# A graph network of four layers: the next entry's neighbour sums moved behind this entry's z sums, z, y and output kept in one tile, the second layer's bias folded into constants

## The chip, the cores and the metric

The kernel runs on one core of a Trainium2 chip. The metric is the device time of one execution in microseconds (us); the profile is one further execution, recorded by the hardware profiler. Engines are named as in the profile: PE is the matrix engine and PEld its weight loads, DVE the vector engine, ACT the scalar engine, POOL GpSimd, SP the sync engine, which here only issues transfers.

## The reference

The input x has 32 entries of 512 nodes by 256 features (float32). adj is one sparse 512 by 512 matrix that all entries share. Four layers follow one another; the first and the last have the same form with weights of their own:

```python
def L0(h):                      # and L3
    pre_u, pre_v = h @ W1[:d], h @ W1[d:]
    S = sigmoid(relu(pre_u[:, u] + pre_v[:, v] + b1) @ W2 + b2)    # one number for each pair u, v
    a_t = einsum('buv,bud->bvd', S * adj, h)
    m_t = einsum('uv,bud->bvd', adj, h) * h
    return beta1 * h + beta2 * (a_t @ Wa + ba) + beta3 * (m_t @ Wm + bm)
def L1(z):
    return z + relu((adj @ z) @ W.T + b)                           # y
def L2(y):
    feats = y @ W1.T
    f1 = feats @ W2 + b2
    coefs = softmax(leaky_relu(f1[:, :, None] + f1[:, None, :]) + adj)
    return coefs @ feats + bias2 + y
```

S is needed only where adj is not zero, so the kernel makes it for the edges alone.

## The kernel before

Entries are worked in eight groups of four (`NB`). Every group passes through five streams of small pieces:

- `first`: turns the four inputs round on PE, writes them to DRAM as `xT`, and writes `pre_u` and `pre_v` of all nodes to a DRAM table (`pre`).
- `edges` of layer 0: 36 items. An item fetches table rows by an indirect transfer (POOL, L612), adds the other node's rows (DVE, L691), applies relu and W2 (DVE L707, or DVE L699 with ACT L677), the sigmoid, and puts the values into a DRAM array `cells` by an indirect transfer (POOL, L606).
- `middle`: the rest of layer 0, layers 1 and 2, and `pre` of layer 3, one entry after the other (`middle_one`).
- `edges` of layer 3, then `last`: the rest of layer 3 and the output.

All streams are woven into one order by `weave`: each piece has a due time on a scale in which a group takes 1.0, and pieces are written out in order of due time. The due times of the middle's pieces are spread by `middle_shares`, a hand-written list of weights; those of the edges by `edge_times`. Pieces of `first` and `last` are "fill": they wait in a list and are written out behind those pieces of the middle that yield True. The framework then arranges the instructions of each engine, mostly in this order; an instruction can be taken ahead of others where its inputs and its buffer are ready by the framework's reckoning. Each engine, and each queue of transfers, then works strictly in its own order.

An entry of `middle_one` consists of these steps, by the lines of the kernel before:

1. `mhT`: 16 PE rows adj x h (L45; a float32 matmul of the code is two rows in the trace) and two DVE products with hT (L755). These are the neighbour sums of the layer.
2. The sums for z: 16 PE rows hWa x `flat` (L845) and 8 rows with mhT (L852); ACT scales hT in place (L850), DVE adds the sums (L853, two instructions). z lies in the tile of hT.
3. zW: 16 PE rows with z as the stationary side (L866), copied by ACT (L870).
4. adj x zW (16 rows, L45), relu with bias by ACT (L876) into `yT`, plus z by DVE (L877).
5. feats (L888, copied by ACT L896 into a tile that shares the tag `mhT0`), a softmax of four chunks (ACT L912 and L916, DVE L913 to L918), four turns (L957), of which two have the next entry's hWa (L744) in front of them in the text, and coefs x feats (16 rows), with the sum x2 by DVE (L935).
6. x2 goes to DRAM (SP, L937). `flat` of the next entry is copied by ACT (L814, four copies) out of `SA`, the four tiles of layer 0's S * adj, into the tile that coefs had. Then `pre` for layer 3 (16 PE rows; DVE L579, ACT L580, DVE L582 and L583 for each of four chunks), and x2 is turned (L946).

`flat` and coefs share one buffer (tag `eT`). h (`h1`), hT (`hT1`), `hWa0` and `mhT0` have one buffer each. At a group's start the text loads SA (POOL, L732), h and hT (SP, L821 and L825), and makes hWa of the first entry. Group 0 is a special case ("given"): its hWa and mhT are made in `middle_before`. PSUM has seven banks for all products (`ps`) and one for f1.

Of the kernel before, what the change touches and what calls it, by code (L numbers as in the profile page):

```python
# [47 lines left out]
class Model:  # L48
# [90 lines left out]
    def others_loads(self, raw):  # L139
        nc, a, const = self.nc, self.a, self.const  # L140
        self.b_1 = self.column("L1_gnn_b")
        self.w2 = self.column("L2_gnn_W2")
        self.b2 = self.bcast("L2_gnn_b2", 1)
        self.bias2 = self.column("L2_gnn_bias2")
        self.W1_1, self.W1_2 = raw([P, DC, D]), raw([P, DC, D])
        nc.scalar.dma_start(self.W1_1, a["L1_gnn_W"].rearrange("(c p) d -> p c d", p=P))
        nc.scalar.dma_start(self.W1_2, a["L2_gnn_W1"].rearrange("(c p) i -> p c i", p=P))
        self.twob2 = const.tile([P, 1], F32, name="twob2")
        self.WT_1 = const.tile([P, DC, D], F32, name="WT_1")
        self.WT_2 = const.tile([P, DC, D + 1], F32, name="WT_2")  # L150

    def others(self, psum):
# [9 lines left out]
        for c in range(DC):  # L162
            pq = psum()[:, 0:1]
            mm(nc, pq, [(self.W1_2[:, r, c * P : (c + 1) * P], self.w2[:, r, :]) for r in range(DC)])
            nc.vector.tensor_copy(self.WT_2[:, c, D : D + 1], pq)
        yield

# [52 lines left out]
class Edges:  # L220
# [28 lines left out]
    def build(self, counts, adjT, lists, psum, big, tmp):  # L249
# [66 lines left out]
        for c in (0, 2, 1, 3):  # L316
            if c == 1:
# [21 lines left out]
                for k in range(2 * PANELS):  # L339
                    if k < 2:  # L340
                        gots.append(two[:, k, :])
                    else:
                        gots.append(tmp.tile([P, 2 * N], F32, name=f"got{k}", tag=("h1", "hT1")[k - 2]))
                    index = bass.IndirectOffsetOnAxis(ap=inode[:, k : k + 1], axis=0)
# [74 lines left out]
class Sparse:  # L419
# [3 lines left out]
    def __init__(self, ctx, m, counts, xr, outr, B):  # L423
# [18 lines left out]
        self.ps_f1 = pool("ps_f1", 1, space=PSUM)  # L442
        self.later, self.bigs, self.given, self.marks = None, 0, None, {}

# [120 lines left out]
    def pre(self, g, b, hT):  # L565
# [3 lines left out]
        for c in range(NC):  # L569
# [10 lines left out]
            nc.scalar.copy(puv[:, 1, :], pp[:, D:])  # L580
            both = self.small.tile([P, D], F32, name="both", bufs=1)
            nc.vector.tensor_tensor(both, pp[:, D:], puv[:, 0, :], ALU.add)  # L582
            nc.vector.scalar_tensor_tensor(  # L583
# [31 lines left out]

    def edges(self, g, spare=()):

# [28 lines left out]
        def fetch(n):  # L646
# [11 lines left out]
            if tag := tags[n % len(tags)]:  # L658
                rows = self.act.tile([P, GROUP], F32, name="rows_more", tag=tag)
            else:  # L660
# [61 lines left out]
        while ready:  # L722
            put()
        yield

# [52 lines left out]
    def middle_before(self, g0, i):  # L778

        self.given = []  # L780
        for b in range(NB):
            h, hT = self.fresh(i + b)
            hT = hT()
            both = self.big(F32, 2048, 3).rearrange("p (k n) -> p k n", k=2)
# [7 lines left out]

    def middle(self, g0, g3, i):


        SA = self.load(g0, 0)
        given, self.given = self.given, None
        h, hT = self.fresh(i, given)
        hT = hT()
        hWa = None  # L800
        if not given:
            for hWa in self.hWa(g0, hT, 0):
                yield
        flat = self.flat(SA, 0)
        for b in range(NB):
            keep = [h, hT, hWa, flat]
            yield from self.middle_one(g0, g3, b, i + b, SA, keep, given)
            h, hT, hWa, flat = keep
        self.settle()
# [6 lines left out]

    def fresh(self, i, given=None):
        h = None
        if not given:
            h = self.act.tile([P, NC, D], F32, name="h1")  # L820
            self.nc.sync.dma_start(h, self.xr[i])  # L821

        def turned():
            hT = self.act.tile([P, DC, N], F32, name="hT1")
            self.nc.sync.dma_start(hT, self.xT[i])  # L825
            return hT

        return h, turned

    def middle_one(self, g0, g3, b, i, SA, keep, given):  # L830
        nc, m, w = self.nc, self.m, g0.w
        act, small, psum = self.act, self.small, self.psum
        h, hT, hWa, flat = keep
        if given:
            hWa, mhT = given[b]
        else:
            for mhT in self.mhT(h, hT, 0):
                yield
        zT = hT
# [8 lines left out]
        for c, pz in enumerate(sums):  # L848
# [5 lines left out]
            yield c == DC - 1  # L854
        more = b < NB - 1
        if more:
            keep[0], turned = self.fresh(i + 1, given)

        zW = act.tile([P, NC, D], F32, name="zW", tag="hWa0")
        halves = [(0, psum()), (2, psum())]  # L860
        for d in range(DC):
# [9 lines left out]
            yield d == DC - 1  # L871
        yT = act.tile([P, DC, N], F32, name="yT")
        for c in range(DC):
            py = psum()
            mm(nc, py, [(zW[:, r, c * P : (c + 1) * P], self.adjT[:, r, :]) for r in range(NC)])
            nc.scalar.activation(yT[:, c, :], py, AF.Relu, bias=m.b_1[:, c, :])  # L876
            nc.vector.tensor_tensor(yT[:, c, :], yT[:, c, :], zT[:, c, :], ALU.add)  # L877
            yield c == DC - 1

        feats = act.tile([P, NC, D + 1], F32, name="feats", tag="mhT0")  # L880
        eT = act.tile([P, NC, N], F32, name="eT")
        if more:
            keep[1] = turned()
            ahead = None if given else self.hWa(g0, keep[1], 0)
        pns = [psum() for _ in range(NC)]
# [14 lines left out]
        fcol = small.tile([P, NC, 1], F32, name="fcol", bufs=1)  # L900
        nc.vector.tensor_scalar(fcol, feats[:, :, D : D + 1], m.twob2, None, ALU.add)
        f1 = self.ps_f1.tile([P, N], F32, name="f1")
# [21 lines left out]
        for ic in (NC - 2, NC - 1):  # L924
            if more and ahead:
                keep[2] = next(ahead)
                yield
            self.put_back(eT, ic, exs[ic])
            yield True
        xT = yT  # L930
        for c in range(DC):
            cs = slice(c * P, (c + 1) * P)
            pv = psum()
            mm(nc, pv, [(feats[:, jc, cs], eT[:, jc, :]) for jc in range(NC)])
            nc.vector.scalar_tensor_tensor(xT[:, c, :], pv, m.bias2[:, c, :], yT[:, c, :], ALU.add, ALU.add)  # L935
            yield c == DC - 1
        nc.sync.dma_start(self.x2T[i], xT)  # L937
        if more:
            keep[3] = self.flat(SA, b + 1)
        yield from self.pre(g3, b, xT)  # L940
# [126 lines left out]

def middle_shares(given):


    hWa = [] if given else [1.7, 1.7]
    shares = list(hWa)
    for b in range(NB):
        more = hWa if b < NB - 1 else []
        shares += [] if given else [2.8, 2.8]
        shares += [3.4, 3.4, 1.0, 2.7]
        shares += [1.7, 3.4, 2.8, 4.5] + [0.9] * NC
        shares += [0.4, 0.4, 0.4, 1.0, 0.4, 1.0] + more + [1.5, 1.5]
        shares += [2.8, 4.5] + [0.4] * NC + [0.5, 0.5]
    return shares + [0.1]  # L1080
# [3 lines left out]
def sparse_path(ctx, m, counts, xr, outr, B):  # L1084
# [10 lines left out]
    for t in range(last + 1):  # L1095
# [17 lines left out]
        if t == last:  # L1113
# [4 lines left out]
            (sp.first(g0, t * NB), first, "fill"),  # L1118
            (sp.edges(g0, ("yT", "mhT0", "hWa0") if t == 0 else ()), edges0, ""),
            (sp.middle(g0, g3, t * NB), spread(middle_shares(t == 0), start, end), "main"),  # L1120
            (sp.edges(g3, ("yT", "h1", "hT1") if t == last else ()), edges3, "free"),
        ]
# [245 lines left out]
```

## Time and profile before

| | |
|---|---|
| three runs | 3113.56, 3114.72, 3128.83 us; median 3114.72 us |
| span of the profiled execution | 3112.8 us (its own execution time is not listed apart from the runs above) |
| busy, share of the span | PE 87%, DVE 74%, POOL 49%, ACT 43%, PE weight loads 53% |
| mean granted PE clock | 0.942 of full speed |
| one group in the steady part | about 358 us; the middle's first sums for z start at 239.8 us, the last entry's coefs x feats ends at 2881.9 us |

A row of the waits names who waited for whom: microseconds in total, times, longest. A row of the groups of instructions gives busy time and the mean of one in ns, then the engine's idle time before it and what ended most of it. In a timeline a bracket at a row's end is the engine's idle time just before it.

### The profile page before, as it was taken

How to read it: one execution, taken by the hardware profiler on the slowest of the kernel's cores; microseconds unless marked ns; L12 is line 12 of the kernel's file. 1: busy time of each engine (PE TensorE's matmuls, PEld its weight loads, DVE VectorE, ACT ScalarE, POOL GpSimd, SP SyncE). 2: the span in 40 equal slices, each digit the busy share in tenths (PEclk: the TensorE clock that was granted, in tenths of full speed). 3: DMA queues.
4: the chain of work that ended last, by engine and by line, in shares of the span. 5: the costliest groups of instructions: out<-in, count | busy, mean ns of one | idle time of the engine just before them, and what ended most of it. 6: DMA issues, size and time to landing. Idle time of an engine off the chain costs nothing. (4 is left out here: it accounts for less than half of the span.)

```text
span 3112.8 us, 32475 instructions
## 1 busy us (share of the span) xinstructions
PE 2713.5 (87%) x8645; PEld 1639.7 (53%) x8646; DVE 2302.9 (74%) x6027; ACT 1337.7 (43%) x4101; POOL 1531.2 (49%) x1328
## 2 busy tenths in 40 slices
PE   6367878889998899989998899989998899879957
PEld 3133444446654566446654565545654466546636
DVE  6964877888689776988489785888679795772761
ACT  3553454444344433444354442544345343443440
POOL 2561553656345552656346562555436563450461
PEclk9688889999999999999999999999999999999979
DMA  8774657776778757776678766787578766551753
GB/s 278 267 238 151 210 164 242 248 261 214 225 214 293 220 189 227 245 263 216 210 212 258 236 196 211 243 266 234 177 225 273 247 220 200 182 183 49 231 196 115
DMA packets 302719, 679.40 MB, mean 218 GB/s; under 512 B 52672, under 2 KB 170944, under 8 KB 294336
## 3 DMA queue, kind: packets, MB, share of 16 engines
q0 software_dynamic: 122688, 414.40, 42.6%
q1 hardware_dynamic: 160880, 225.62, 22.0%
q10 hardware_dynamic: 18960, 37.24, 3.2%
q8 instruction: 70, 1.15, 0.1%
q14 instruction: 121, 0.99, 0.1%
HBM read 531.12 MB, written 146.01 MB: 218 GB/s over the span
## 5 line engine op out<-in xcount | busy, mean ns | idle before, releaser
L606 POOL DMA_INDIRECT cells<-s,cell x576 | 686.4, 1192 | 747.0 <-DMA cells<-s,cell 388.5
L612 POOL DMA_INDIRECT rows<-table,iv x552 | 667.6, 1209 | 619.9 <-DMA table<-puv 150.5
L691 DVE TENSOR_TENSOR rows<-rows,mine 128x1024 f32<-128x1024 f32 x552 | 667.4, 1217 | 191.7 <-DMA rows<-table,iv 173.3
L677 ACT ACTIVATE rows<-rows 128x256 f32<-128x256 f32 x1088 | 439.8, 407 | 506.6 <-DVE rows L699 477.3
L45 PE MATMUL pst<-adj,h 128*128 128x512 f32 x1024 | 452.6, 594 | 0.3 <-PE pst L946 0.3
L707 DVE SCALAR_TENSOR_TENSOR rows<-rows,L_gnn_W2bc 128x256 f32<-128x256 f32 x1120 | 415.0, 417 | 1.8
L45 PE MATMUL pst<-L_gnn_Wa,hT 128*128 128x256 f32 x1024 | 261.3, 406 | 104.8 <-DMA hT<-xT 56.2
L699 DVE SCALAR_TENSOR_TENSOR rows<-rows,L_gnn_W2bc 128x1024 f32<-128x1024 f32 x272 | 329.7, 1214 | 0.3
L45 PEld LDWEIGHTS pst<-adj,h 128*128 128x128 f32 x1024 | 193.4, 191 | 223.3 <-issue 219.4
L45 PEld LDWEIGHTS pst<-L_gnn_Wa,hT 128*128 128x128 f32 x1024 | 204.8, 205 | 151.8 <-issue 85.1
L45 PE MATMUL pst<-eT,feats 128*128 128x512 f32 x512 | 230.9, 604 | 13.0 <-ACT eT L958 13.0
L866 PE MATMUL pst<-WT,hT 128*128 128x256 f32 x512 | 155.1, 470 | 96.0 <-DVE hT L853 96.0
L45 PE MATMUL pst<-adjT,zW 128*128 128x512 f32 x512 | 227.7, 597 | 3.8 <-ACT zW L870 3.8
L1006 PEld LDWEIGHTS pst<-hWa,SA 128*128 128x128 f32 x896 | 213.8, 328 | 7.7 <-issue 4.1
L1006 PE MATMUL pst<-hWa,SA 128*128 128x256 f32 x896 | 216.8, 398 | 0.0
L814 ACT COPY flat<-SA 128x512 f32<-128x512 f32 x128 | 137.7, 1127 | 165.9 <-PE pst L45 83.7
L677 ACT ACTIVATION_READ_ACCUMULATOR rows<-rows 128x1 f32 x1088 | 205.4, 189 | 0.0
L845 PE MATMUL pst<-flat,hWa 128*128 128x512 f32 x448 | 196.8, 592 | 0.0
L866 PEld LDWEIGHTS pst<-WT,hT 128*128 128x128 f32 x512 | 121.4, 242 | 136.6 <-DVE hT L853 107.1
L579 DVE TENSOR_TENSOR puv<-pst,bc_L_gnn_b 128x256 f32<-128x256 f32 x256 | 104.4, 414 | 95.8 <-DMA table<-puv 58.6
L580 ACT COPY puv<-pst 128x256 f32<-128x256 f32 x256 | 93.5, 370 | 180.6 <-DVE puv L579 162.7
L45 PEld LDWEIGHTS pst<-eT,feats 128*128 128x128 f32 x512 | 97.2, 193 | 127.5 <-issue 109.4
(172 smaller groups left out, 3984.4 us busy)
## 6 DMA issues: line engine op xcount, KB each, us to landing
table<-puv SPq DMA_DIRECT2D x256, 256.0 KB, 5.7
SA<-cells POOLq DMA_DIRECT2D x64, 1024.0 KB, 7.2
h<-in_x_dram SPq DMA_DIRECT2D x64, 512.0 KB, 6.5
mine<-table SPq DMA_DIRECT2D x64, 512.0 KB, 5.5
hT<-xT SPq DMA_DIRECT2D x36, 512.0 KB, 5.0
h<-x2s SPq DMA_DIRECT2D x36, 512.0 KB, 4.4
xT<-hT ACTq DMA_DIRECT2D x32, 512.0 KB, 6.1
x2T<-yT SPq DMA_DIRECT2D x32, 512.0 KB, 5.5
```

What stands on the lines that cost most here:

```text
L45: nc.tensor.matmul(out, lhsT, rhs, start=(n == 0), stop=(n == len(pairs) - 1))
L579: nc.vector.tensor_tensor(puv[:, 0, :], pp[:, 0:D], w["b1bc"], ALU.add)
L606: self.nc.gpsimd.indirect_dma_start(out=g.cells[half], out_offset=bass.IndirectOffsetOnAxis(ap=at, axis=0), in_=s, in_offset=None)
L612: self.nc.gpsimd.indirect_dma_start(out=rows, out_offset=None, in_=g.table, in_offset=bass.IndirectOffsetOnAxis(ap=at, axis=0))
L677: self.behind(nc.scalar.activation(part, part, AF.Identity, accum_out=g.s[:, k, b : b + 1]))
L691: self.behind(nc.vector.tensor_tensor(rows, rows, other, ALU.add))
L699: nc.vector.scalar_tensor_tensor(by_entry, by_entry, 0.0, w2, ALU.max, ALU.mult)
L707: nc.vector.scalar_tensor_tensor(part, part, 0.0, w["W2bc"], ALU.max, ALU.mult, accum_out=at)
L814: self.nc.scalar.copy(flat[:, r, :], SA[r][:, :, b])
L845: nc.tensor.matmul(pz, hWa[:, r, cs], flat[:, r, :], start=(r == 0), stop=False)
L866: nc.tensor.matmul(pw[:, at], zT[:, d, cs], m.WT_1[:, d, :], start=(d + k == 0), stop=(d * k == 1))
L1006: nc.tensor.matmul(pz[:, k * D : (k + 1) * D], SA[r][:, cs, b], hWa[:, r, :], start=(r + k == 0), stop=False)
```

## The change

- The generator `made_ready` holds the next entry's loads of h and hT, its mhT and its hWa. `middle_one` takes two pieces of it (mhT) between L853 and L866, and two more (hWa) in front of the last two turns of the softmax. This goes on across groups: the last entry of a group makes the first entry of the next ready, so that a group's start has no hWa and mhT of its own. In group 0 only its last entry does so.
- `hT1` has two buffers. y is written over z and the output over y; `yT` is no tile of its own, and `feats` has one.
- y is kept without its bias: z + max(sums, -b) by one DVE instruction straight from PSUM, in place of L876 and L877. The missing b is put back through two constants, `bias2y` and `twob2y`, made once.
- `both` of `pre` lies in PSUM in place of an SBUF tile.
- SA of layer 0 is loaded at the end of the stream `edges` in place of the start of `middle`.
- `middle_shares` has new weights.

```diff
+        self.nb_1 / self.bias2y / self.twob2y: const tiles
@@ others
+        nc.vector.tensor_scalar(self.nb_1, self.b_1, -1.0, None, ALU.mult)
+        nc.vector.tensor_tensor(self.bias2y, self.bias2, self.b_1, ALU.add)
+        for c in range(DC):
+            pq = psum()[:, 0:1]
+            mm(nc, pq, [(self.WT_2[:, r, c * P : (c + 1) * P], self.b_1[:, r, :]) for r in range(DC)])
+            nc.vector.tensor_tensor(self.bias2y[:, c, :], self.bias2y[:, c, :], pq, ALU.add)
+        pq = psum()[:, 0:1]
+        mm(nc, pq, [(self.WT_2[:, r, D : D + 1].to_broadcast([P, P]), self.b_1[:, r, :]) for r in range(DC)])
+        nc.vector.scalar_tensor_tensor(self.twob2y, pq, 2.0, self.twob2, ALU.mult, ALU.add)
@@ pre
-            both = self.small.tile([P, D], F32, name="both", bufs=1)
-            nc.vector.tensor_tensor(both, pp[:, D:], puv[:, 0, :], ALU.add)
+            both = pp[:, D:]
+            nc.vector.tensor_tensor(both, both, puv[:, 0, :], ALU.add)
@@ edges
+        if layer == 0:
+            g.SA = self.load(g, 0)
         yield
@@ new functions
+    def turned_of(self, i):
+        hT = self.act.tile([P, DC, N], F32, name="hT1", bufs=2)
+        self.nc.sync.dma_start(hT, self.xT[i])
+        return hT
+    def made_ready(self, g0, i):
+        h, hT = self.fresh(i)
+        for mhT in self.mhT(h, hT, 0):
+            yield
+        for hWa in self.hWa(g0, hT, 0):
+            yield hT, hWa, mhT
@@ middle
-        SA = self.load(g0, 0)
-        h, hT = self.fresh(i, given)
-        if not given:
-            for hWa in self.hWa(g0, hT, 0):
-                yield
+        SA = g0.SA
         flat = self.flat(SA, 0)
         for b in range(NB):
...
+            ahead = None if given or (last and b == NB - 1) else self.made_ready(g0, i + b + 1)
+            yield from self.middle_one(g0, g3, b, i + b, SA, ready, flat, ahead, got)
@@ middle_one
-            for mhT in self.mhT(h, hT, 0):
-                yield
+        hT, hWa, mhT = ready
...
-        if more:
-            keep[0], turned = self.fresh(i + 1, given)
+        if ahead:
+            for _ in range(DC):
+                next(ahead)
+                yield
...
-        yT = act.tile([P, DC, N], F32, name="yT")
+        yT = zT
-            nc.scalar.activation(yT[:, c, :], py, AF.Relu, bias=m.b_1[:, c, :])
-            nc.vector.tensor_tensor(yT[:, c, :], yT[:, c, :], zT[:, c, :], ALU.add)
+            nc.vector.scalar_tensor_tensor(yT[:, c, :], py, m.nb_1[:, c, :], zT[:, c, :], ALU.max, ALU.add)
-        feats = act.tile([P, NC, D + 1], F32, name="feats", tag="mhT0")
+        feats = act.tile([P, NC, D + 1], F32, name="feats")
...
-            if more and ahead:
-                keep[2] = next(ahead)
+            if ahead:
+                got["ready"] = next(ahead)
                 yield
...
-            nc.vector.scalar_tensor_tensor(xT[:, c, :], pv, m.bias2[:, c, :], yT[:, c, :], ALU.add, ALU.add)
+            nc.vector.scalar_tensor_tensor(xT[:, c, :], pv, m.bias2y[:, c, :], yT[:, c, :], ALU.add, ALU.add)
@@ middle_shares
-        shares += [] if given else [2.8, 2.8]
-        shares += [3.4, 3.4, 1.0, 2.7]
-        shares += [1.7, 3.4, 2.8, 4.5] + [0.9] * NC
-        shares += [0.4, 0.4, 0.4, 1.0, 0.4, 1.0] + more + [1.5, 1.5]
-        shares += [2.8, 4.5] + [0.4] * NC + [0.5, 0.5]
+        shares += [3.4, 3.4, 1.7, 1.7] + ([3.4, 3.4] if ahead else [])
+        shares += [1.7, 2.4, 3.4, 4.0] + [0.9] * NC
+        shares += [0.4, 0.4, 0.4, 1.0, 0.4, 1.0] + ([1.7, 1.5, 1.7, 1.5] if ahead else [1.5, 1.5])
+        shares += [3.4, 4.0] + [1.7] * NC + [0.5, 0.5]
```

## The prediction

> **What bounds the kernel now.** I read the busy shares first, then the waits of PE, the groups of instructions, and timelines of single entries. The busy shares name PE, with DVE next:
>
> ```profile
> PE 2713.5 (87%) x8645; PEld 1639.7 (53%) x8646; DVE 2302.9 (74%) x6027; ACT 1337.7 (43%) x4101; POOL 1531.2 (49%) x1328
> ```
>
> PE is idle for 3112.8 − 2713.5 = 399 us. By the timeline about 118 of them lie before the middle of group 0 (set-up) and 53 behind the last middle; neither stretch is bound by what is changed. The other 228 us lie inside the eight middles. The waits of PE say where:
>
> ```profile
> PE pst L866 <- DVE hT L853: 96.0, 22, 9.5
> ...
> PE pst L957 <- DVE ex L918: 41.0, 23, 8.3
> PE pst L957 <- DVE cols L917: 29.1, 5, 6.6
> ...
> PE pst L888 <- DVE yT L877: 5.9, 6, 1.8
> ```
>
> The largest is L866, the product zW, which waits for z. The groups of instructions show that this wait costs more than itself; columns are busy us and mean ns, then idle time:
>
> ```profile
> L866 PE MATMUL pst<-WT,hT 128*128 128x256 f32 x512 | 155.1, 470 | 96.0 <-DVE hT L853 96.0
> L888 PE MATMUL pst<-WT,yT 128*128 128x257 f32 x512 | 117.9, 381 | 5.9 <-DVE yT L877 5.9
> ```
>
> Two products of one size take 470 and 381 ns. The timeline of entry 10 shows why: sums for z, wait, zW.
>
> ```profile
> 1001.83 7.03 PE L845 MATMUL pst<-flat,hWa 128*128 128x512 f32 x16
> 1008.69 3.60 PE L852 MATMUL pst<-mhT,L_gnn_Wm 128*128 128x512 f32 x8
> 1012.13 1.89 PE L45 MATMUL pst<-L_gnn_Wa,hT 128*128 128x256 f32 x8
> 1023.54 6.70 PE L866 MATMUL pst<-WT,hT 128*128 128x256 f32 x16 [9.53 <-DVE hT L853]
> ```
>
> zW takes 6.70 us here and 3.62 in entry 11, which did not wait; by windows the clock is 0.79 in 1008 to 1032 us and 1.00 in 1095 to 1113. The sums were complete at 1012, so what held z is DVE's own order:
>
> ```profile
> 1012.37 0.16 DVE L632 TENSOR_TENSOR self_s<-self_s,diag 128x16 f32<-128x16 f32 x1
> 1021.67 1.22 DVE L691 TENSOR_TENSOR rows<-rows,mine 128x1024 f32<-128x1024 f32 x1 [9.14 <-DMA rows<-table,iv]
> 1022.81 0.68 DVE L853 TENSOR_TENSOR hT<-hT,pst 128x512 f32<-128x512 f32 x1
> ```
>
> DVE stood at an edge item whose rows had not landed, and L853 was queued behind it.
>
> **The change part by part.** Entries counted from 0, waits at L866 from the timeline, group 0 (unchanged there) left out: second entries of groups (5, 9, 13 and so on) 23.6 us, DVE busy with a backlog; third entries (6, 10, 14 ...) 50.2, the DVE stall above; first entries (4, 12, 16 ...) 19.6, DVE waiting for the first rows of layer 3; fourth entries 0. Sum 93.4. zW's excess over 3.62 us, summed over the entries, is 39.3.
>
> *mhT behind the sums for z.* It adds no PE work. An mhT row group lasts 7.03 us, so the sums for z reach DVE 7 us earlier in an entry, while PE comes to zW no earlier. And L853 moves up in DVE's order. By the due times worked out from the two lists of weights, L853 of a third entry stood behind the seventh edge item of layer 0 (0.576 against 0.569 of the group) and will stand behind the third (0.529 against 0.520). In a second entry it moves from item 24 to item 20 of layer 3, in a first entry from behind three items to ahead of the first. So the first entries' 19.6 should go whole. Of the third entries' 50.2 what exceeds 7 us may stay (8.5): 41.7 go. Where DVE is the limit (94% busy in 900 to 1000 us) time freed comes back, so I count half of 23.6: 11.8. Sum −73.
>
> *The clock.* With these waits goes most of the 39.3; I take −31 in proportion (73 of 93). [...]
>
> *y.* L876 (64 x 682 ns on ACT) and L877 (64 x 686 on DVE) give way to one DVE instruction reading PSUM; the nearest row is L935, of the same kind and shape, 736 ns: DVE +3.2 us, ACT −43.6, both beside PE. PE's wait at L888 (5.9) goes: −6. Without PE's cover the shorter chain would be worth 0.7 us a time.
>
> *hWa in the fourth entries.* Moved from the group's start into the softmax, 3.5 us of work that in entry 3 meets a wait of 5.1; elsewhere PE is full there: −3.
>
> *`both` in PSUM.* [...] I take 0 on DVE. The bank is held for L583 as well, half a us longer; PE's waits on L582 for a bank are 22.1 us in all, 15.9 of them in set-up. Between −0 and +10 us; I take +3. The new constants are six short products and five small DVE instructions in set-up, beside the building of the edge lists: 0 to 2 us, I take +1.
>
> *Transfers on SP.* Loads of h and hT (6.5 and 5.0 us to landing) move from 25 to 80 us ahead of their use to about 10, behind x2T's store and four table writes on the in-order SP queue; second buffers of hT let the load start when x2T(i−1) has been stored. SP can take a load ahead of its place: one of h was issued at 1090.8, its group beginning at 1170. If all 28 are late by 2 us, 56; if none, 0. I take +6. Queued behind a late h are PE's mhT and all after it.
>
> *SA.* On POOL the four loads move from the middle's start to the end of layer 0's edges, past a few fetches only; they wait for the last values put:
>
> ```profile
> 1519.89 2.15 ACT L814 COPY flat<-SA 128x512 f32<-128x512 f32 x2 [7.77 <-PE pst L45]
> 1527.96 1.13 ACT L814 COPY flat<-SA 128x512 f32<-128x512 f32 x1 [5.93 <-DMA SA<-cells]
> 1530.88 1.09 ACT L814 COPY flat<-SA 128x512 f32<-128x512 f32 x1 [1.78 <-DMA SA<-cells]
> ```
>
> Here `flat` is complete 12 us after coefs x feats ends. Before, hWa and mhT (10.5 us) filled PE until the sums for z; now only `pre`, the turns and one fill do, 9.5 us, plus 1.3 until the fourth tile is used: at least 1 us of wait. The new weights also put coefs x feats 0.019 of a group (6.7 us) earlier against the edges' end. So the wait at L845 is between 0 and 8 us at each of seven group starts, more if the edges hold the pace; I take 5: +35. Inside a group `flat` was ready 10 to 13 us before use, less 7 now, so no wait.
>
> Sum: −73 −31 −6 −3 +3 +1 +6 +35 = −68 us on the profiled 3112.8, 1.9 below the median of the runs. From 3114.7 that is 3047 us.
>
> **Rivals.** *A, the forecast.* For it: L866 is PE's largest wait, with a clock penalty; PE has no spare work there.
>
> *B, more.* If DVE's edge work slides behind the softmax too, a part of the 70 us at L957 goes, and SA costs nothing: −68 −35 −15 = about 2997. Against it: 94% DVE.
>
> *C, the stall only moves.* DVE's 9 us without rows stay, since the rows come from POOL and DMA; PE then stops at L888 or at the next entry's mhT, or the framework puts mhT elsewhere than the text does. Gain 0 to 30: 3085 to 3115. For it: DVE waits for rows for 173 us in all.
>
> *D, slower: the edges' end sets the pace.* The place is L845 at the group's start: sums for z wait for the last SA tile through `flat`, and ACT, in order, holds `pre`'s banks meanwhile. Without the 35, the sum is −103. At 103 / 7 = 15 us a group the gain is gone, and 20 us give 3112.8 − 103 + 140 = 3150, with the median's 2 us 3152. For it: SA already lands 8 to 12 us after coefs x feats, and the puts before it go one by one, about 5 us each. Against it: POOL idles 21 us at that point waiting for tables, and edges are partly held back only by PE's own waits in DVE's order.
>
> **How the numbers follow.** A 0.50 (3015 to 3085), B 0.15 (2985 to 3015), C 0.11 (3085 to 3115), D 0.24 (3131 to 3200). A measurement of this kernel tells about 0.5% (15.6 us) from no change. Faster: A, B and a small part of C, 0.67; same: the rest of C, 0.09; slower: D, 0.24. The range 2990 to 3150 leaves out a part of B and half of D. A's own range is 3015 to 3085.
>
> **What would show it.** Right: L866 near 380 ns with under 25 us of wait, the clock above 0.95, an L45 adj x h group between L852 and L866, no L876, the new L877 near 736 ns. The sum's weakest term is L845: a wait on `flat` under 50 us keeps A, over 100 means D. PE waiting at L45 for the transfer of h would show the SP term mis-sized. Wrong altogether: waits at L866 as before though mhT stands there, or edges that end later against coefs x feats.

## The result, and the profile after

The changed kernel takes 3160.93 us (median of 4 runs, 3158.93 to 3171.95); the kernel before, run beside it, 3115.59 us (4 runs). The ratio is 1.0141 with a 95% interval of 1.0108 to 1.0174: slower by 45 us, where 68 us less were forecast. The profiled execution spans 3159.3 us against 3112.8, at a mean granted clock of 0.930 against 0.942.

The page's first row after the change: PE is busier by 25 us (2713.5 before), although its work grew by 12 short instructions only.

```profile
PE 2738.7 (87%) x8657; PEld 1649.3 (52%) x8658; DVE 2315.3 (73%) x6032; ACT 1295.9 (41%) x4037; POOL 1527.1 (48%) x1328
```

Line numbers moved: zW L866 is now L882, y's instruction is L892, feats L888 is L900, the turns of the softmax L957 are L972, the sums for z L845 are L860, z's addition L853 is L868, the edge items' addition L691 is L703. The waits of PE after (us in total, times, longest):

```profile
PE pst L900 <- DVE hT L892: 72.2, 14, 7.2
PE pst L972 <- DVE ex L930: 65.1, 29, 6.4
PE pst L860 <- ACT flat L846: 46.0, 2, 37.6
...
PE pst L972 <- DVE cols L929: 33.3, 6, 7.7
PE pst L860 <- ACT puv L592: 28.6, 6, 5.8
```

The 96.0 us at zW are gone (0.6 us are left). In their place PE waits 72.2 us for y, where it waited 5.9; 98.4 us in the softmax instead of 70.1; and 28.6 us at the sums for z of six groups' starts (L592, ACT's copies of `pre`), where it had no wait before. These four together were 172 us and are 200 us. The two waits for `flat` stand ahead of group 0 (37.6 us, in set-up) and inside it (8.4), not at the group starts that the prediction meant. The two products of one size have changed roles, in mean ns as in waits:

```profile
L882 PE MATMUL pst<-WT,hT 128*128 128x256 f32 x512 | 117.0, 380 | 0.8 <-DVE hT L868 0.6 <-issue 0.2
L900 PE MATMUL pst<-WT,hT 128*128 128x257 f32 x512 | 140.5, 432 | 72.2 <-DVE hT L892 72.2
```

A row of the windows, around one wait for y from 1783 to 1794 us (length, busy times of PE, PEld, DVE, ACT and POOL, then the granted clock, here 0.66):

```profile
1783.00:1794.00 11.00, 5.98 (x12) 3.53 (x11) 7.97 (x21) 2.83 (x11) 4.66 (x5) 0.66 0.91 341
```

zW gave back 38.1 us of PE time (155.1 to 117.0), feats took 22.6 of it (117.9 to 140.5), coefs x feats as much again (230.9 to 253.5). The timeline of a third entry, the counterpart of entry 10 before:

```profile
1748.81 3.60 PE L867 MATMUL pst<-mhT,L_gnn_Wm 128*128 128x512 f32 x8
1752.25 7.03 PE L45 MATMUL pst<-adj,h 128*128 128x512 f32 x16
1759.11 3.62 PE L882 MATMUL pst<-WT,hT 128*128 128x256 f32 x16
...
1778.65 3.79 PE L900 MATMUL pst<-WT,hT 128*128 128x257 f32 x8 [5.60 <-DVE hT L892]
...
1790.46 3.79 PE L900 MATMUL pst<-WT,hT 128*128 128x257 f32 x8 [5.02 <-DVE hT L892]
```

```profile
1754.99 0.68 DVE L868 TENSOR_TENSOR hT<-hT,pst 128x512 f32<-128x512 f32 x1
...
1769.56 1.23 DVE L703 TENSOR_TENSOR rows<-rows,mine 128x1024 f32<-128x1024 f32 x1 [9.20 <-DMA rows<-table,iv]
...
1777.86 0.74 DVE L892 SCALAR_TENSOR_TENSOR hT<-pst,nb,hT 128x512 f32<-128x512 f32 x1
...
1785.99 1.23 DVE L703 TENSOR_TENSOR rows<-rows,mine 128x1024 f32<-128x1024 f32 x1 [4.94 <-DMA rows<-table,iv]
```

The forecast's picture came true: mhT stands behind the sums, L868 stands ahead of DVE's stall, zW starts without a wait. But the stall itself is as long as before (9.20 us, it was 9.14). It now stands ahead of y's first instruction, together with 7 us of edge items that piled up behind it, and a second stall of 4.94 us stands ahead of y's second instruction. PE stops some 20 us later in the entry than before, twice, for 10.6 us. The third entries of groups 1 to 6 all look like this: a stall of 8.5 to 9.6 us, then one of 4.5 to 6.3 us.

Where the time went, from one group's first sums for z to the next: set-up 239.8 and 240.0 us; group 0 245.6 and 238.9; groups 1 to 6 together 2130.4 and 2190.2; the last group 265.9 and 259.7. All of the loss, 60 us, lies in the six groups of the steady part, 10 us a group on average (2.5 to 17); the first and the last group together won 13 us. Over groups 2 to 6, called the steady groups from here on, PE idles 30.7 us a group instead of 25.0 and is busy 336.4 instead of 332.1, with the same work at a lower granted clock (0.96 against 0.97 there).

### The profile page after: what moved, and what is told of

It reads as the page before. It is cut to its first block, busy times and chain, and to the rows that moved or that the text cites. A ratio compares the mean times of both kernels' runs of the same rounds, so it can differ in the third digit from the quotient of the medians.

```text
span 3159.3 us, 32112 instructions
## 1 busy us (share of the span) xinstructions
PE 2738.7 (87%) x8657; PEld 1649.3 (52%) x8658; DVE 2315.3 (73%) x6032; ACT 1295.9 (41%) x4037; POOL 1527.1 (48%) x1328
## 5 line engine op out<-in xcount | busy, mean ns | idle before, releaser
L703 DVE TENSOR_TENSOR rows<-rows,mine 128x1024 f32<-128x1024 f32 x552 | 667.0, 1217 | 173.8 <-DMA rows<-table,iv 153.4
L45 PE MATMUL pst<-adj,h 128*128 128x512 f32 x1024 | 462.6, 602 | 9.9 <-DMA h<-in_x_dram 9.9
L45 PE MATMUL pst<-eT,feats 128*128 128x512 f32 x512 | 253.5, 653 | 23.0 <-ACT eT L973 21.9
L587 PE MATMUL pst<-w_L_gnn_W,hT 128*128 128x512 f32 x512 | 250.5, 614 | 26.4 <-ACT hT L574 20.9
L589 PE MATMUL pst<-w_L_gnn_W,hT 128*128 128x512 f32 x512 | 248.9, 598 | 0.0
L860 PE MATMUL pst<-flat,hWa 128*128 128x512 f32 x448 | 207.3, 617 | 28.6 <-ACT puv L592 28.6
L900 PE MATMUL pst<-WT,hT 128*128 128x257 f32 x512 | 140.5, 432 | 72.2 <-DVE hT L892 72.2
L45 PEld LDWEIGHTS pst<-eT,feats 128*128 128x128 f32 x512 | 105.5, 210 | 156.8 <-issue 123.6
L972 PE MATMUL pst<-ident,ex 128*128 128x128 f32 x512 | 91.1, 312 | 99.0 <-DVE ex L930 65.1
```

Of the source, the lines that this page charges most:

```text
L45: nc.tensor.matmul(out, lhsT, rhs, start=(n == 0), stop=(n == len(pairs) - 1))
L587: nc.tensor.matmul(pp, hT[:, 0, ks], w["W1"][:, 0::DC, :], start=True, stop=False)
L589: nc.tensor.matmul(pp, hT[:, 1, cs], w["W1"][:, 1::DC, :], start=False, stop=True)
L703: self.behind(nc.vector.tensor_tensor(rows, rows, other, ALU.add))
L860: nc.tensor.matmul(pz, hWa[:, r, cs], flat[:, r, :], start=(r == 0), stop=False)
L900: nc.tensor.matmul(pn[:, 0 : D + 1], yT[:, r, ic * P : (ic + 1) * P], m.WT_2[:, r, :], start=(r == 0), stop=(r == DC - 1),)
```

## The experiments

Theories, by the names that the expectations use. T1: the new stall at a group's start is the loss. T2: the new weights put the middle's instructions at worse places among the edges' on DVE. T3: a side edit (y, `both`, SA's place) is the loss. T4: PE's waits only move, because DVE with its edge items sets the pace; T4a by its own backlog, T4b because it hands on late rows. T5: late rows come from the order of POOL's queue. T6: all is in balance, and a wait taken away comes back elsewhere. T8: POOL's puts as a whole set the pace. The kernel before ran beside each; its median was 3101 to 3105 us, and 3120 beside the two kernels named "rows_first".

**Side edits (T3).** y alone in the kernel before, with the folded bias:

```diff
-            nc.scalar.activation(yT[:, c, :], py, AF.Relu, bias=m.b_1[:, c, :])
-            nc.vector.tensor_tensor(yT[:, c, :], yT[:, c, :], zT[:, c, :], ALU.add)
+            nc.vector.scalar_tensor_tensor(yT[:, c, :], py, m.nb_1[:, c, :], zT[:, c, :], ALU.max, ALU.add)
```

> Theory 1 (the time is lost at the group's start, where PE waits at the sums for z for ACT, 5.6 us and a cold clock behind it; the other waits of PE only move): this kernel has y by one DVE instruction and the folded bias alone, so 3105 to 3118 us, no change or a little faster than before. Theory 2 (the new weights put the middle's DVE instructions too early among the edges'): the same. Theory 3 (the side edits cost the time): 3130 to 3160.

3107.41 us, 1.002 [0.9997, 1.0043]. `both` alone, in the kernel before:

```diff
-            both = self.small.tile([P, D], F32, name="both", bufs=1)
+            both = pp[:, D:]
```

> The kernel before with the sums of pre kept in PSUM, nothing else changed. Theory 3, what is left of it after the kernel with y alone ran at 1.002 (banks are held longer, or DVE is slower on PSUM): 1.005 to 1.02. Theories 2 and 4: 0.997 to 1.004, and the second instruction of the pair at 418 to 430 ns.

3106.38 us, 1.0017 [0.9999, 1.0034]. The row that grew most on DVE is the reading of the accumulator behind L583, first before, then in this kernel:

```profile
L583 DVE DVE_READ_ACCUMULATOR both<-both,L_gnn_W2bc 128x1 f32 x256 | 20.5, 80 | 0.0
```

```profile
L583 DVE DVE_READ_ACCUMULATOR pst<-pst,L_gnn_W2bc 128x1 f32 x256 | 35.9, 140 | 0.0
```

L582 and L583 themselves take 430 and 427 ns, 13 and 9 more than before. But the rows of a timeline overlap, and the reading lies under its neighbours; one place of before, then the same place here:

```profile
915.17 0.43 DVE L583 SCALAR_TENSOR_TENSOR both<-both,L_gnn_W2bc 128x256 f32<-128x256 f32 x1
915.52 0.08 DVE L583 DVE_READ_ACCUMULATOR both<-both,L_gnn_W2bc 128x1 f32 x1
915.52 0.68 DVE L755 TENSOR_TENSOR mhT<-pst,hT 128x512 f32<-128x512 f32 x1
```

```profile
916.74 0.42 DVE L583 SCALAR_TENSOR_TENSOR pst<-pst,L_gnn_W2bc 128x256 f32<-128x256 f32 x1
917.08 0.14 DVE L583 DVE_READ_ACCUMULATOR pst<-pst,L_gnn_W2bc 128x1 f32 x1
917.08 0.69 DVE L755 TENSOR_TENSOR mhT<-pst,hT 128x512 f32<-128x512 f32 x1
```

From the start of L583 to the start of what follows it without a gap, DVE takes 347 ns on average before and 346 here, and its busy time is 2302.9 us before and 2303.3 here: the longer rows cost DVE nothing. SA's load put back to the middle's start, in the changed kernel:

```diff
-        if layer == 0:
-            g.SA = self.load(g, 0)
-        SA = g0.SA
+        SA = self.load(g0, 0)
```

> The changed kernel with SA of layer 0 loaded at the start of the middle again. Theories 2 and 4: no change against the changed kernel, a ratio of 1.010 to 1.020 to before. If the place of the loads on POOL matters: outside that.

3149.20 us, 1.0136 [1.0097, 1.0175], as with the change whole. This run is a repeat of the changed kernel: PE, DVE, ACT, POOL and SP work in the same order in both traces, the loads included. In the kernel before, too, two of a group's four loads already stand among the last puts and two behind them. So this edit is no cause of the loss, but another place of the loads was not tried. T3 is out for y and `both`. The second buffer of hT, y's place over z, and the places of the loads of h and hT were not tried alone, but PE has no wait on those loads in the steady groups.

**The group's start (T1).** In the changed kernel each group makes hWa and mhT of its first entry at its own start again:

```diff
+        if not given and not ready:
+            for ready in self.made_ready(g0, i):
+                yield
...
-            ahead = None if given or (last and b == NB - 1) else self.made_ready(g0, i + b + 1)
+            ahead = None if was_given or b == NB - 1 else self.made_ready(g0, i + b + 1)
```

> The changed kernel, but each group makes mhT and hWa of its first entry itself at its start; inside a group mhT stays between z and zW. Theory 1: the wait at a group's start goes, about 8 to 9 us in each of seven groups, so 3095 to 3115 us. Theory 2: 3145 to 3165, since DVE's order inside the groups is as in the change. Theory 3: 3145 to 3165.

3143.80 us, 1.0152 [1.0107, 1.0196]. And `flat` held behind the copies of `pre` on ACT at a group's start, so that the wait on L592 is taken away:

```diff
+                self.tc.add_manual_dep(ins.ins, held, order, reason="behind the sums' copies")
```

> The changed kernel, but at a group's start ACT's four copies of flat are ordered behind the copies of pre, so that a late SA no longer holds the banks and tables of pre. Theory 1: PE no longer waits there for ACT's puv, the tables of layer 3 go out about 10 us earlier, and part of the wait passes to flat itself: 3105 to 3135 us. Theory 2: 3145 to 3165. Theory 3: 3145 to 3165.

3141.19 us, 1.0125 [1.0068, 1.0181]. The waits of PE of the first, then of the second:

```profile
PE pst L589 <- DVE hT L954: 52.5, 6, 10.0
...
PE pst L45 <- ACT zW L890: 42.3, 8, 7.3
```

```profile
PE pst L863 <- ACT flat L846: 73.6, 11, 33.2
```

In both the wait on `puv` at the sums for z is gone and the loss is not. In the first PE now waits for x2 and for zW's copy. In the second the wait passed to `flat` itself: 41.1 of the 73.6 us stand in set-up and group 0, as in the changed kernel, and 32.5 at and behind the later groups' starts, so that run alone decides nothing. By the first, T1 falls: the 28.6 us are a place where lateness shows, not its source.

**Place and weights (T2).** mhT at the entry's end, with the rest of the change:

```diff
-            for _ in range(DC):
-                next(ahead)
-                yield
...
             nc.scalar.dma_start(self.x2s[i][:, c : c + 2, :], x2)
             yield
+        if ahead:
+            for got["ready"] in ahead:
+                yield
```

> The changed kernel, but mhT of the next entry is made at the end of an entry, behind the turns of x2, in place of between z and zW. Theory 1: mhT covers the copies of flat again, the wait at the sums for z goes, and waits at zW come back: 3105 to 3125 us. Theory 2: the weights are as in the change, so 3145 to 3170. Theory 3: 3145 to 3165.

3216.97 us, 1.0375 [1.0339, 1.0412]: PE waits 107.0 us for z again and 105.8 for `flat`, 44.7 of them in set-up and group 0. Within the change, mhT between z and zW is worth 2.3% against this place (1.0375 / 1.0141). That is not the worth of the place by itself: the kernel before with the new weights has its mhT between x2 and the sums for z as well and stands at 1.0153 (below), so at this place the rest of the change costs some 2%. The 61.1 us for `flat` at later groups' starts, which that kernel does not have, are a part of it; the rest was not taken apart. The changed kernel with the weights of before, and the kernel before with the new ones:

```diff
-        shares += [3.4, 3.4, 1.7, 1.7] + ([3.4, 3.4] if ahead else [])
-        shares += [1.7, 2.4, 3.4, 4.0] + [0.9] * NC
-        shares += [3.4, 4.0] + [1.7] * NC + [0.5, 0.5]
+        shares += [3.4, 3.4, 1.0, 2.7] + ([2.8, 2.8] if ahead else [])
+        shares += [1.7, 3.4, 2.8, 4.5] + [0.9] * NC
+        shares += [2.8, 4.5] + [0.4] * NC + [0.5, 0.5]
```

> The changed kernel with the weights of before (mhT 2.8, 2.8 now standing behind the sums for z). Theory 1 (a fixed stall at the group's start) fell with the kernels that hold flat back and that make a group's first entry at its start. Theory 2 (the new weights give the middle's instructions the wrong places among the edges' on DVE): a ratio of 0.96 to 0.995 to before. Theory 4 (DVE and the fetched rows set the pace of a group, and PE's waits only move): 1.005 to 1.02 as in the change.

3111.22 us, 1.0035 [1.0019, 1.0050].

> The kernel before with the weights of the change (mhT 3.4, 3.4 at the entry's start). Theory 2: the weights alone make it slower, a ratio of 1.015 to 1.04. Theory 4: 0.995 to 1.01, since no work and no wait is added.

3145.14 us, 1.0153 [1.0127, 1.0178]. And of the new weights only that of `pre`, taken back in the changed kernel:

```diff
-        shares += [3.4, 4.0] + [1.7] * NC + [0.5, 0.5]
+        shares += [3.4, 4.0] + [0.4] * NC + [0.5, 0.5]
```

> The changed kernel with one number set back: the weight of a piece of pre, 0.4 in place of 1.7. The other new weights of an entry sum to the same as the old ones (28.5 up to coefs x feats). If pre's weight is what costs (it leaves room for edge items between pre's chunks on DVE, and moves all that stands before it earlier among the edges): a ratio of 1.000 to 1.006, as with all old weights. If the other weights cost: 1.010 to 1.016.

3113.73 us, 1.0041 [1.0025, 1.0058]. The loss has two parts, then. The weights cost 1.0% in the changed kernel and 1.5% in the kernel before; in the changed one, taking back the single weight of `pre` (0.4 to 1.7 for each of four pieces) recovers nearly all of that. And the new order with old weights gains nothing. The waits of PE, first of the changed kernel with old weights, then of the kernel before with new ones:

```profile
PE pst L972 <- DVE ex L930: 69.4, 30, 5.4
...
PE pst L900 <- DVE hT L892: 41.5, 20, 5.8
PE pst L972 <- DVE cols L929: 32.7, 6, 6.4
```

```profile
PE pst L866 <- DVE hT L853: 67.0, 23, 9.1
PE pst L957 <- DVE ex L918: 61.9, 31, 9.1
...
PE pst L888 <- DVE yT L877: 30.1, 10, 5.7
PE pst L957 <- DVE cols L917: 18.0, 3, 7.3
```

With old weights PE idles 25.4 us a steady group with 6.1 us of waits for z at zW in the whole kernel, where the kernel before idles 25.0 with 96.0. The second fence shows the same exchange without mhT being moved at all: new weights take 29 us from zW's wait (96.0 to 67.0) and add 24 at y (5.9 to 30.1) and 10 in the softmax (70.1 to 79.9).

**Less work on DVE (T4a against T4b).** In three kernels relu and W2 of an edge item run over 64 of 256 features:

```diff
-                by_entry = rows.rearrange("p (b d) -> p b d", b=NB)
+                by_entry = rows.rearrange("p (b d) -> p b d", b=NB)[:, :, 0:64]
```

> The kernel before with the relu-and-W2 instruction of each edge item on 64 of 256 features, so that the sums for S are incomplete; transfers, ACT and PE as before. It takes some 0.8 us of DVE from each of 576 items. Theory 4a (DVE's own backlog is what PE waits for): the wait at zW falls under 40 us, a ratio of 0.955 to 0.975. Theory 4b (DVE only hands on the lateness of the fetched rows): the wait at zW stays over 60 us, a ratio of 0.98 to 1.00.

The kernel before: 3065.47 us, 0.9879 [0.9856, 0.9902]. zW and feats in it:

```profile
L866 PE MATMUL pst<-WT,hT 128*128 128x256 f32 x512 | 118.1, 384 | 8.5 <-DVE hT L853 8.5
L888 PE MATMUL pst<-WT,yT 128*128 128x257 f32 x512 | 119.8, 386 | 8.6 <-DVE yT L877 8.6
```

The wait at zW is gone here without a move of mhT (96.0 to 8.5 us), zW is at 384 ns, and y did not take the wait over. In the waits this is what T4a said (under 40 us), in the time what T4b said. For a smaller part of this wait and its low clock the forecast took 104 us (73 and 31) off the time; here they went almost whole, with some DVE work besides, and the time fell by 38 us (between the two profiled spans 45: 62 less in the eight groups, 16 more in set-up).

> The changed kernel with the weights of before, and the same lightening of DVE as in the kernel before. Theory 4a: with DVE no limit any more, the place of mhT counts as forecast, and it runs 1 to 3 per cent below the lightened kernel before. Theory 4b: within 0.7 per cent of it, the waits standing at y and in the softmax.

The changed kernel with old weights: 3088.19 us, 0.9951 [0.9931, 0.9970].

> The changed kernel with its own weights and the same lightening of DVE. Theory 4a: the weights matter little once DVE has room, within 0.7 per cent of the lightened kernel with old weights. Theory 4b: still 1 to 1.5 per cent above it.

The changed kernel: 3129.47 us, 1.0086 [1.0058, 1.0115]. In the kernel before, DVE's idle time in a steady group rises from 75 to 123 us, and the group gets 5 us shorter. DVE's backlog is not what swallowed the gain: with it gone, the new order should have run 1 to 3% below the old one and runs 0.7% above it, and the new weights still cost 1.3%, as T4b said. T4a falls. (With the shorter instructions the framework also set DVE's, ACT's and POOL's rows in another order, so these three kernels change more than DVE's load.) What DVE waits for most is rows: 281 us in the first and third of these kernels, 215 in the second, against 173 before.

**POOL's queue.** In the kernel before, the rows that DVE lacks in a third entry stand behind puts, each of which waits for the landing of the one before:

```profile
1364.06 1.79 POOL L606 DMA_INDIRECT cells<-s,cell  x1 [3.88 <-DMA cells<-s,cell]
...
1369.24 1.19 POOL L606 DMA_INDIRECT cells<-s,cell  x1 [2.81 <-DMA cells<-s,cell]
1372.77 0.98 POOL L606 DMA_INDIRECT cells<-s,cell  x1 [2.34 <-DMA cells<-s,cell]
1374.05 1.01 POOL L612 DMA_INDIRECT rows<-table,iv  x1 [0.30 <-ACT hWa L745]
```

```profile
1380.31 1.23 DVE L691 TENSOR_TENSOR rows<-rows,mine 128x1024 f32<-128x1024 f32 x1 [8.75 <-DMA rows<-table,iv]
```

A first attempt to change that order gave later due times to layer 3's last puts:

```diff
-        edges3 = edge_times(end + 0.003, end + 0.05, end + 0.48, end + 0.54)
+        edges3 = edge_times(end + 0.003, end + 0.05, end + 0.48, end + 0.575)
```

> The kernel before, with one number changed: the last values of layer 3's edges are put at due times spread to 0.575 of a group behind the middle's end instead of 0.54, so that on POOL's queue the row fetches of layer 0's next edges come between them and not behind them; the orders on PE, DVE and ACT stay as they are. T5 (POOL's queue is what holds the rows: a fetch stands behind a run of puts, each of which waits some 4 to 5.5 us for the one before it, and DVE's 9 us stall in each third entry is that fetch): the stall at the edge item ahead of the sums' addition in the third entries falls from about 9 us to under 4, zW's wait there with it, and the steady group gets 5 to 9 us shorter: ratio 0.983 to 0.992. T6 (puts, fetches and the other engines are in balance, what is taken away at one place comes back at the next): the stall moves to another item of layer 0's edges, ratio 0.997 to 1.003.

> The changed kernel with the sums for the next layer weighted as before (0.4) and the last puts of layer 3's edges spread in the same way. Without the spread it stood at 1.004 to the kernel before. T5: with the rows in time the third entries' waits at the product y and at zW's copy go, and now also what the new place of mhT saves can be seen: ratio 0.975 to 0.988, below that of the kernel before with the same spread. T6: 0.998 to 1.006, as without it. If it gains just as much as the kernel before does, the place of mhT is worth nothing whether or not the rows are late.

> The changed kernel as it is (weight 1.7 for the sums for the next layer) with the last puts spread. Without the spread 1.014. T5: 1.000 to 1.008; if the weights cost what they cost only by way of late rows, the distance to the kernel with the old weight shrinks from 1% to under 0.4%. T6: 1.010 to 1.018.

1.0010 [0.9990, 1.0029], 1.0036 [1.0021, 1.0051] and 1.0178 [1.0143, 1.0213]. These decide nothing between T5 and T6: the framework wrote POOL's queue out in the same order as without the edit, so the three tell how well a ratio repeats (within 0.1% of the unedited kernel's for two, 0.4% for the third). With an explicit order between a put and the newest fetch, on top of the later due times, POOL's queue does change, while PE and ACT keep theirs:

```diff
+                newest = next(reversed(self.fetch_of))
+                if late and newest is not g:
+                    self.tc.add_manual_dep(ins.ins, self.fetch_of[newest].ins.name, order, reason="behind the rows")
```

> The kernel before, with the last puts of layer 3's edges made to stand behind the newest row fetches of layer 0's next edges on POOL's queue: before the last such put 11 fetches of the next table are issued where it was 7, and what PE, DVE and ACT do stands in the same order as before. (In the three kernels with a spread tail POOL's order had stayed as it was, so they tell only how far a repeat scatters: 1.001, 1.0036 and 1.0178 where the originals stand at 1, 1.0041 and 1.0141.) T5 (a fetch behind waiting puts is what DVE, and through it PE, waits for in the third entries): DVE's stall on rows around 200 us into a group falls from about 9 us to under 4, zW's wait there from 9 to under 4, ratio 0.983 to 0.993. T6 (balance: the wait comes back elsewhere): the stall goes, or moves, and the ratio is 0.997 to 1.004. If the puts themselves become late, layer 0's edges end later and z's sums at the group's start wait: over 1.005.

3122.52 us, 0.9999 [0.9980, 1.0018]. zW and feats in this kernel, where L872 was L866 and L894 was L888:

```profile
L872 PE MATMUL pst<-WT,hT 128*128 128x256 f32 x512 | 144.2, 444 | 50.5 <-DVE hT L859 50.5
L894 PE MATMUL pst<-WT,yT 128*128 128x257 f32 x512 | 133.8, 415 | 51.1 <-DVE yT L883 51.0
```

Half of zW's wait is taken away (96.0 to 50.5), and the same 45 us appear at y (5.9 to 51.1). The stall of 9 us has become two, of some 3 and 5 us. This is the result of the change once more, brought about on POOL alone.

> The changed kernel with the sums for the next layer weighted as before (0.4), and the same order of puts and fetches on POOL's queue; PE and ACT in the same order as without it, DVE with one item moved by a place or two. Without it 1.004 to the kernel before. T5: the waits at zW's copy and at y in the third entries (about 10 us of 25 in a group) go, ratio 0.970 to 0.990, lower than that of the kernel before with the same order. T6: 1.000 to 1.007. Should both kernels gain alike, late rows cost time but did not swallow the change's gain.

3124.70 us, 1.0016 [0.9998, 1.0035]. T5 falls. The last run leaves half of the puts out, so that SA lacks half of the edges' values, in the changed kernel with the old weight of `pre`; PE, DVE and ACT keep work and order:

```diff
                 j = e.order[k]
+                if k % 4 > 1:
+                    continue
                 ready.append((e.half_of(j), e.cell[:, j : j + 1], g.s[:, k, :]))
```

> The changed kernel with the sums for the next layer weighted as before (0.4), and half of the edge values never put into the cells (of every four items two are left out, so SA lacks them); PE, DVE and ACT do the same work in the same order, only POOL's queue has 288 puts fewer, each of them some 1.2 us of issue and often a wait of 3 to 5 us for the put before it. With all puts it stands at 1.004. T8 (POOL's queue sets the group's pace: its two edge stages fill the group but for 25 us): the stalls on rows fall, the group gets shorter by 8 to 15 us, ratio 0.965 to 0.985. T6 (the wait comes back elsewhere whatever is taken away): 0.996 to 1.006, with the stall on rows shorter and others longer. Between, 0.985 to 0.996: POOL holds a part.

3010.73 us, 0.9699 [0.9683, 0.9715], against 1.0041 with all puts: T8's range (0.965 to 0.985), not T6's. The puts on POOL and DVE's wait for rows, with all puts and then with half:

```profile
L618 POOL DMA_INDIRECT cells<-s,cell x576 | 687.7, 1194 | 644.9 <-DMA cells<-s,cell 425.7 <-issue 91.8 <-DVE s L653 56.5
...
DVE rows L703 <- DMA rows<-table,iv: 167.4, 62, 11.5
```

```profile
L618 POOL DMA_INDIRECT cells<-s,cell x288 | 360.2, 1251 | 357.1 <-DVE s L653 173.4 <-DMA cells<-s,cell 79.5 <-issue 50.0
...
DVE rows L705 <- DMA rows<-table,iv: 64.3, 31, 8.0
```

Of the 95 us between the two profiled spans 66 lie in the eight groups (8.3 us in a steady one) and 29 in set-up and behind the last middle. PE's wait at y falls from 28.7 us to 1.8, and its idle time in a steady group from 25.1 to 19.0 us. This is the only thing taken away that shortened the groups by more than DVE's lightening did. The puts hold a good part of the pace; not all of it: in each group some 79 us are gone from POOL's queue (an estimate: 36 puts of 1.2 us, and an eighth of the 288 us by which POOL's idle time before the puts fell), and the group is 8.3 us shorter. The bytes that all transfers moved hardly differ (679.4 and 678.7 MB), so the volume is not what was relieved; whether it is POOL's queue alone or also the 3% fewer packets (302716 to 293497) is not separated. Whether the new order pays in such a kernel is not told by this run, as the kernel before was not run with half of the puts.

No version that does the whole work was faster than the kernel before.

## Why the prediction was wrong

**The step that failed** is the first term, "Sum −73", in the words "of the third entries' 50.2 what exceeds 7 us may stay (8.5): 41.7 go". It took a wait that PE would no longer have at zW for time that the kernel would no longer take. The wait went fully, 95 us of it, even in the second entries where only half was counted. But what PE waited behind, DVE's stalls at edge items whose rows are late, stayed: DVE's place in its order moved, and a stall as long now precedes y. The kernel with old weights shows it without the weights' cost: 25.4 us of PE's idle time a steady group against 25.0. Rival C had this ("PE then stops at L888") and was given 0.11; its range was a gain of 0 to 30 us, and that kernel lost 0.35%. Of the signs of being right all but the clock came true while the time rose; none of them looked at PE's idle time over a whole group.

**The clock, −31.** It fell with the same step. zW did become as fast as said (380 ns); the low clock went to feats in the third entries (635 ns a row in the one shown, at a clock of 0.50 from 1778.6 to 1782.4 us; 432 ns on average over all entries) and to coefs x feats in the second entries, behind the softmax's waits, 10.08 us at a clock of 0.70 here where the same entry before takes 7.13 at 1.00:

```profile
1715.22 1.08 PE L972 MATMUL pst<-ident,ex 128*128 128x128 f32 x4 [4.56 <-DVE ex L930]
...
1722.92 0.68 PE L972 MATMUL pst<-ident,ex 128*128 128x128 f32 x4 [3.21 <-DVE ex L930]
1724.28 10.08 PE L45 MATMUL pst<-eT,feats 128*128 128x512 f32 x16 [0.68 <-ACT eT L973]
```

The mean clock went down to 0.930; above 0.95 was forecast.

**y, −6, and hWa, −3.** y's instruction takes 746 ns (736 forecast). Alone the new y brought +0.2% with an interval down to −0.03%, so nothing of the −6 (−0.2%) can be seen. hWa was not tried alone.

**`both`, +3.** The time agrees (+5 us, with an interval from 0 to 11, by the ratio), and so does the 0 taken for DVE, whose busy time grew by 0.4 us. Two rows of before bear that 0: L582, which reads PSUM, took 417 ns, and L583, all in SBUF, 418. With `both` in PSUM the row of L583 is 9 ns longer, and the next instruction starts no later (346 ns against 347).

**SP, +6.** Mis-sized to the safe side: PE has no wait on a transfer of h or hT in the steady groups.

**SA and the start, +35.** The wait came in the forecast's size, 28.6 us for 35, on L592 in place of `flat`: the step holds as a description and fails as a cost. With that wait gone the time was the same (1.0152). The loads of SA, which the prediction let move past fetches on POOL, moved by two puts at most and past no fetch. The time fell into rival D's range, but by luck: edges that end late do hold PE at the group's start (2.4 to 5.8 us at each of six), and that is not what costs.

**The weights** were priced only as part of that term ("0.019 of a group earlier"). By the runs they cost more than all the rest of the change: 1.0 to 1.5%, 31 to 47 us. That they cost this much in the kernel before as well, where no SA is waited for, shows that they act on the whole weave. How is not shown. A layer 3 edge stage, from its first fetch to its last put on POOL's timeline, lasts 186 us on average before and 198 with the new weights, 187 and 199 in the changed kernel with the old and the new weight of `pre`; but with all old weights it lasts 195 there, at no loss, so its length alone is not the cause. Open too is what else, beside POOL's puts and DVE's edge work, holds the 19 us that PE still idles in a group with half of the puts.

One reading of the prediction was off, without weight: inside the eight middles PE idled 236 us before the change, not 228; the 12.6 us for `flat` inside group 0 were counted as set-up.

## What to carry to other kernels

When in-order queues are woven together and the trace shows a wait of PE behind a DVE instruction that itself stands behind a late transfer (9.53 us at zW in entry 10, behind 9.14 us of DVE without rows), moving PE's work into that wait may only hand the stall to the next product, as here (95 us less at zW, 66 more at y); before counting such a wait as gain, ask what the late transfer stands behind, and try on the chip what the time does when that is taken away; an edit of due times or of an instruction's place in the text counts as tried only when the queue's rows stand in another order. Weights that set the order for all streams are an edit of their own: run them alone in the old kernel, because one number of them here made 1.0 of the 1.4% that the whole change lost. A sum of waits that falls at one line is no gain until PE's idle time over the whole group has fallen.

## What the runs showed of the hardware

- The row of an accumulator's reading is 140 ns behind an instruction on PSUM and 80 ns behind the same one on SBUF (427 and 418 ns), but it lies under its neighbours: from the instruction's start to the next one's, DVE took 346 ns with PSUM and 347 with SBUF. Summed over 256 times, what the rows of the reading, L582 and L583 grew by (60, 13 and 9 ns) would be 21 us; DVE's busy time grew by 0.4.
- In the kernel before, zW's 16 rows of entry 10, behind a wait of 9.53 us, took 796 ns, then 634 each for twelve rows, 564 at the turn, then 380 and 379. How many were slow up to the turn does not follow the wait's length: 12 behind 3.34 us (entry 12), 6 behind 5.03 (entry 22), 8 behind 8.78 (entry 26), 13 behind 9.53 (entry 10), none behind 2.84 (entry 24, its first row 483 ns).
- A chained put waits 2.3 to 3.9 us for the landing of the one before it in the fence above; with half of the puts the waits on landing fell from 425.7 to 79.5 us, far more than by half, and all idle time before the puts from 644.9 to 357.1.
